# A fused macaron block in fp32: the last attention projections and one more kept pair as Strassen-Winograd block products

## The chip, the cores and the metric

The kernel runs on one core of a Trainium2 chip. The metric is the device time of one execution in microseconds; lower is better. Several executions are timed and the median is given.

## The reference

Four sequences of 1024 tokens with 1024 channels, all in fp32: 4096 tokens, or 32 tiles of 128. A gated feed-forward part is added with half weight, then attention, then the same feed-forward part again. Cut to what matters:

```python
def ffn(x):                                  # x: 4096 x 1024
    dots = softmax(x @ centroids.T / 0.1)    # 64 clusters
    hits = dots > 0.01
    dense = x @ weight.T + bias              # 1024 x 1024
    row_sel = any(hits, axis=0)[assignments] # which output columns are kept
    return where(any(hits, axis=1)[:, None] & row_sel[None, :], dense, 0)

def attn(x):                                 # 32 query heads, 8 key/value heads, width 32
    q, k, v = x @ Wq + bq, x @ Wk + bk, x @ Wv + bv
    k, v = repeat(k, 4), repeat(v, 4)
    scores = einsum('bsdh,bseh->bsde', q, k) / sqrt(32)
    return einsum('bsde,bseh->bsdh', softmax(scores), v)

x = x + 0.5 * ffn(layernorm(x))
x = x + attn(layernorm(x))
x = x + 0.5 * ffn(layernorm(x))
```

The scores of a token are taken between its own channels d and e, summed over the heads; no token attends to another one. A column is kept only if some token anywhere hits its cluster, so the mask of each feed-forward part is known only when all 32 tiles have been through its gate.

## The kernel before

The work is in tiles of 128 tokens. `wc` holds W.T and the centroids side by side, 1024 + 64 columns; the last part of a product (columns 768 to 1088, 320 wide) holds the last 256 outputs and the 64 logits of the gate. `wqkv` holds the projection, 768 columns, the four query heads of a group already summed.

There are three stages, in an order of instructions that is written out by hand: each engine executes its own in the order of the program.

The first stage makes the first feed-forward part and stores its rows in DRAM (`d1`). The second is the loop over `s` from 0 to 36 (line 982), a software pipeline. I call one pass *step s*. In it tile s is projected, tile b = s - 2 has its scores (L877), softmax and weighted sum (`attend`, L919), tile g = s - 3 gets the attention added by GpSimd (`second_added`, L944 and L948) and its layernorm moments by VectorE (L162), tile f = s - 4 is transposed for the last part (L205), and tile a = s - 5 goes through the gate (`gate_2`: a product of 320 columns, L212). The third stage makes the rest of the last feed-forward part and writes the result.

Two tiles can share a matrix product in the Strassen-Winograd form: their rows are split into halves over the contraction, and the weights into four blocks of 512 x 384. Seven products of blocks then do the work of eight. `project_two` (L801) does so for the projections of the steps in `PAIRED`, `winograd` (L284) for the feed-forward part. Both are generators: each `next` emits one product and its adds, so that they can be interleaved with other work. They need sums of token blocks (`token_sums`, four GpSimd instructions at L257 to L260) and of weight blocks (`weight_sums`, L245).

The weight sums of the projection (`qts`) lie in the first 768 columns of `wc`, so W.T itself waits in DRAM (`wtd`) and comes back by four transfers on SP's queue (L989), each of 768 KB. Before, two are issued at the top of step 29 and two at the top of step 30. The weight sums of the last feed-forward part (`ts`) in turn lie in `wqkv`, and VectorE makes them in steps 32 and 33.

The six last tiles, 26 to 31, are *kept*: their x, xT and feed-forward rows stay on the chip. Tiles 26 and 27 are finished by `rest` in steps 32 and 33, one tile in each by two plain products; 28/29 by `winograd` in steps 34 and 35, 30/31 in stage 3.

Some orders matter here. All products of this stage but scores and weighted sums take their PSUM bank from one tag of four (`bank`). Scores and weighted sums share one buffer (`att`). In a paired odd step the gathers of the new tile (`rearranged`, L845 and L851) stand ahead of the attention's store (L935) and return (L940) on SP's queue; in an unpaired step behind. In an odd paired step whose follower is also paired, two gates run; in the others after the start, one. The gates are closed by this:

```python
def gates_used():
    for a in sorted(es):
        gated(es.pop(a), a, 1)
```

It runs in each odd or unpaired step, ahead of the softmax.

Of the kernel before, what the change touches and what calls it, by code (L numbers as in the profile page):

```python
# [33 lines left out]
KEPT = 6  # L34
LAST = 2 * HALF, (EMB + NCL) // 2 - HALF
GATED = range(8, 28)
PAIRED = range(4, 30)
WARM = 16
ROWS = 26

# [2 lines left out]
def kernel(  # L43
# [39 lines left out]
    nc = tc.nc  # L83
    xf = x.flatten_outer_dims()
    of = out.flatten_outer_dims()
    NT = xf.shape[0] // P
# [20 lines left out]
    for base, sign in ((0, 1), (HKV - 1, -1)):  # L107
        nc.gpsimd.affine_select(
            out=tq,
            in_=tq,  # L110
# [9 lines left out]
    wc = const.tile([P, KT, EMB + NCL], F32, name="wc")  # L120
# [14 lines left out]
    xt, dt_, xT = {}, {}, {}  # L135
# [79 lines left out]
    def ffn_part(src, i, dst, name, biased=True):  # L215


        lo, hi = PARTS[i]
        p = product(src, wc, lo, hi, f"ff_{name}_{i}")
        hi = min(hi, EMB)  # L220
        if biased:
            nc.vector.tensor_tensor(dst[:, lo:hi], p[:, : hi - lo], brow[:, lo:hi], ALU.add)
        else:
            nc.scalar.copy(dst[:, lo:hi], p[:, : hi - lo])
        return p[:, hi - lo : hi - lo + NCL] if i == 2 else None

    def rest(t):

        for i in range(2):
            ffn_part(xT[t], i, dt_[t], f"3_{t}")  # L230
        del xT[t]

    def blocks(wts, lo=0, n=HALF):

        return [
            wts[:, 4 * i : 4 * i + 4, lo + h * n : lo + (h + 1) * n] for i in (0, 1) for h in (0, 1)
        ]

    def weight_sums(ws, ts, engines):

        w11, w12, w21, w22 = ws
        t1, t2, t3, t4 = ts
        sums = (t1, w12, w11), (t2, w22, t1), (t3, w22, w12), (t4, w21, t2)
        for engine, (o, p, q) in zip(engines, sums):
            engine.tensor_tensor(o, p, q, ALU.subtract)  # L245
            yield
# [214 lines left out]
    def first_added(t):  # L461
        masked(dt_[t], t, 0, mask)
        nc.gpsimd.tensor_tensor(xt[t], xt[t], dt_.pop(t), ALU.add)  # L463
# [6 lines left out]
    with (  # L470
# [5 lines left out]
        ts = [stage.tile([P, 4, HALF], F32, tag=f"ws{i}", name=f"ws{i}") for i in range(4)]  # L476
# [286 lines left out]
    with (  # L763
# [129 lines left out]
        def weighted(s, t, between=lambda: None):  # L893


            st = attn.tile([P, NBLK, 4, D], F32, tag="stt", name=f"stt{t}")
            nc.vector.transpose(
                st.rearrange("p b t d -> p (b t d)"), s.rearrange("p b t e -> p (b t e)")
            )
            between()  # L900
            sm = small.tile([P, 2, 4, 4], F32, tag="asm", name=f"asm{t}")
            nc.vector.tensor_reduce(
                sm.rearrange("p m i t -> p i m t"),
                s.rearrange("p (i m) t e -> p i m t e", m=2),
                AX.X,
                ALU.add,
            )
            rs = small.tile([P, D], F32, tag="rs", bufs=3, name=f"rs{t}")
            nc.vector.transpose(rs, sm.rearrange("p m i t -> p (m i t)"))
            nc.vector.reciprocal(rs, rs)  # L910
            return st, rs
# [44 lines left out]
        def has(t):  # L956
            return 0 <= t < NT
# [13 lines left out]
        def gate_2(a):  # L971
            if a not in dt_:
                dt_[a] = row(f"d3_{a}")
            es[a] = gate(ffn_part(xT[a], 2, dt_[a], f"3_{a}", biased=a >= FIRST_KEPT), a, 1)
# [4 lines that stand above are left out]
                if a < FIRST_KEPT:  # L979
                    store_2(a)  # L980

        for s in range(NT + 5):
            b, g, f, a = s - 2, s - 3, s - 4, s - 5
            paired, odd = s in PAIRED, s % 2 == 1
            if has(s + 4):
                load_2(s + 4)
            for i in {PAIRED.stop - 1: (0, 1), PAIRED.stop: (2, 3)}.get(s, ()):

                nc.sync.dma_start(out=blocks(wc)[i], in_=wtd[i])  # L989
            if has(b):  # L990
                sc = scores(qkv[b][0], kd.pop(b), b)
            if has(b):
                nc.scalar.activation(sc, sc, AF.Exp, scale=QK_SCALE)
            if paired:
                if not odd:
                    two = project_two(s, s + 1, ss2)
                next(two)
            if has(s + 1) and s + 1 not in xT2:
                xT2[s + 1] = transposed(xn2.pop(s + 1), f"2_{s + 1}")
            if has(s - 1):  # L1000
                kd[s - 1] = keys(qkv[s - 1][0], s - 1)
            if has(g):
                second_added(ot.pop(g), rs.pop(g), g)
            if g >= 0 and g < FIRST_KEPT:
                nc.gpsimd.dma_start(out=y2[g], in_=xt[g])
            if odd or not paired:
                gates_used()
            if 3 <= s <= 4:
                next(qsums)
            if has(s + 2):  # L1010
                normal = sums_normed(xt[s + 2], f"2_{s + 2}")
                next(normal)
            if paired and not odd:
                next(two)
            if has(b):
                st, rs[b] = weighted(sc, b, lambda: next(two) if paired and odd else None)
            if paired and not odd:
                first_added(s + 3)
                next(two)
            if has(s + 2):  # L1020
                xn2[s + 2] = next(normal)
            if paired and not odd:
                next(two)
            if paired and odd and s + 1 in PAIRED:
                gate_2(a)
                xT[f] = transposed(xn3.pop(f), f"3_{f}")
            if paired and (not odd or s + 1 not in PAIRED):
                fo = attend(st, qkv.pop(b)[1], b)
            if s == NT + 2:
                dt_[a] = row(f"d3_{a}")  # L1030
                steps = winograd(s - 6, s - 5, ss, ts, None, 3)
                for _ in range(3):
                    next(steps)
            if has(g):
                mv = moments(xt[g], f"3_{g}")

            def between():
                if has(s + 3) and s + 3 in dt_:
                    first_added(s + 3)
                if has(g):  # L1040
                    xn3[g] = normed(xt[g], mv, f"3_{g}")

            if paired:
                if not odd:
                    next(two)
                between()
            elif has(s):
                flat[s] = project(xT2.pop(s), s, between)
            else:
                between()  # L1050
                k = s - NT
                if k < 2:
                    rest(s - 6)
                    if k == 0:
                        sums = weight_sums(blocks(wc), ts, [nc.vector] * 4)
                    for _ in range(2):
                        next(sums)
                if k > 2:
                    load_xT(k - 3)
                if 2 <= k < 4:  # L1060
                    for _ in range(1 if k == 2 else 3):
                        next(steps)
            if paired and odd:
                qkv[s] = rearranged(flat.pop(s), s)
            if has(b) and b in qkv:
                fo = attend(st, qkv.pop(b)[1], b)
            if s in flat:
                qkv[s] = rearranged(flat.pop(s), s)
            if has(b):
                ot[b] = returned(fo, b)  # L1070
            if has(s - 1):
                qkv[s - 1] = (qkv[s - 1][0], values(qkv[s - 1][1], s - 1))
            if has(f) and f in xn3:
                xT[f] = transposed(xn3.pop(f), f"3_{f}")
            if odd and s + 1 in PAIRED:
                xT2[s + 2] = transposed(xn2.pop(s + 2), f"2_{s + 2}")
                ss2 = token_sums(xT2, s + 1, s + 2, "2q")
            if 1 <= s <= 3:

                for _ in range(2 if s == 1 else 1):  # L1080
                    next(held[s // 2])
                i = {1: NT - 4, 3: NT - 2}.get(s)
                for i in (i, i + 1) if i else ():
                    nc.sync.dma_start(out=d1[i], in_=dt_.pop(i))
            if s == 1:
                next(qsums)
            if s == NT + 1:
                ss = token_sums(xT, f - 1, f, 2)
                asg = load_assigned()
            if s == NT + 3:  # L1090
                hot = one_hot(asg)
            if paired:
                if odd:
                    gate_2(f if s + 1 in PAIRED else a)
            elif has(a) and a not in es:
                gate_2(a)
            for i in sorted(es) if odd or not paired else ():
                es[i] = gate_exp(es[i], i, 1)
# [118 lines left out]
```

## Time and profile before

| | us |
|---|---|
| median of 3 runs | 1323.7 (1322.91 to 1324.2) |
| the profiled execution | 1323.88 |
| its span | 1322.2 |
| TensorE busy | 1301.0 |
| VectorE busy | 871.0 |
| GpSimd busy | 583.3 |
| ScalarE busy | 495.1 |
| step 29 begins (scores on TensorE) | 941.22 |
| step 32 begins | 993.12 |
| step 33 begins | 1010.98 |
| step 34 begins | 1028.72 |

Times in the rows are microseconds from the span's start. A row of a timeline gives the start, the length, the engine (PE is TensorE, DVE VectorE, ACT ScalarE, POOL GpSimd, SPq the DMA issues of SyncE), the line of the kernel, the operation, what it writes and reads, and how many instructions are merged in it; in brackets stands the idle time of the engine just before, with what ended it. An fp32 matmul of the program is two instructions in the rows, so a product of four blocks shows as x8.

### The profile page before, as it was taken

Reading aid. Unit: us, or ns where it says so; the run is one execution under the profiler, and the core shown is the slowest. Engines: PE = TensorE matmul, PEld = TensorE weight load, DVE = VectorE, ACT = ScalarE, POOL = GpSimd, SP = SyncE. Lnnn points to the kernel's source line nnn. Section 1 sums busy time; section 2 is a strip of 40 time slices with the busy share of each in tenths; the row PEclk is TensorE's granted clock in tenths of the full one; section 3 lists DMA queues with packets and bytes.
Section 4 is the critical chain, followed back from the end, with each engine's and each line's share of the span. In section 5 each row is a group of like instructions: output and inputs, shape, how many; then the busy total and the mean of one; then the engine's idle time right before and its main releaser. Section 6 shows DMA issues by size and latency. Waiting matters only on the chain.

```text
span 1322.2 us, 22786 instructions
## 1 busy us (share of the span) xinstructions
PE 1301.0 (98%) x8726; PEld 840.5 (64%) x8726; DVE 871.0 (66%) x1789; ACT 495.1 (37%) x821; POOL 583.3 (44%) x448
## 2 busy tenths in 40 slices
PE   8998999999999999999999999999999999999998
PEld 7664677777776665666666666666666655555554
DVE  4655555555546358888888888778867448555556
ACT  4432223333210445666666666666643200000000
POOL 3621132232112147566666666666532326634440
PEclk9999899999999999999999999999999999999999
DMA  8487876778614155456666665665551346655532
GB/s 297 86 161 146 170 146 139 167 180 173 124 64 191 43 166 160 153 191 189 195 200 195 189 198 166 200 200 189 163 156 26 104 139 227 239 200 176 178 114 80
DMA packets 296301, 214.25 MB, mean 162 GB/s; under 512 B 240064, under 2 KB 255168, under 8 KB 296192
## 3 DMA queue, kind: packets, MB, share of 16 engines
q1 hardware_dynamic: 278240, 164.78, 46.5%
q0 software_dynamic: 8736, 30.68, 6.3%
q10 hardware_dynamic: 9216, 17.33, 3.6%
q8 instruction: 69, 1.13, 0.4%
q14 instruction: 40, 0.33, 0.1%
HBM read 127.77 MB, written 84.96 MB: 161 GB/s over the span
## 4 chain that ended last, share of the span: by engine, by line
PE 93%; DMA 2%; DVE 2%; ACT 1%; issue 1%; POOL 0%; SPq 0%; ACTq 0%; POOLq 0%; DVEq 0%
PE st L284 40%; PE qs L801 18%; PE ff L212 16%; PE la L348 6%; PE tp L205 4%; PE pq L212 4%; PE sc L877 2%; PE po L919 2%; DMA x<-in_L_attn_x_dram 1%; DVE bn L162 1%; DMA scd<-sc 1%; PE tpw L558 0%; DMA qkvd<-qkv 0%; DMA xb<-in_L_attn_x_dram 0%; DVE d L275 0%
## 5 line engine op out<-in xcount | busy, mean ns | idle before, releaser
L212 PE MATMUL ff<-wc,xT 128*128 128x320 f32 (+1 forms) x768 | 218.1, 438 | 1.7 <-ACT wc L563 0.7
L212 PEld LDWEIGHTS ff<-wc,xT 128*128 128x128 f32 x768 | 143.7, 190 | 64.1 <-ACT xT L206 1.0
L257 POOL TENSOR_TENSOR ts<-xT 128x512 f32<-128x512 f32 x31 | 41.4, 1335 | 309.6 <-DVE xT L509 172.7
L284 PE MATMUL st<-wc,xT 128*128 128x384 f32 x496 | 170.5, 487 | 0.0
L275 DVE TENSOR_TENSOR d<-st,d 128x384 f32<-128x384 f32 x157 | 86.1, 550 | 109.8 <-PE st L284 108.5
L284 PE MATMUL st<-ws,ts 128*128 128x384 f32 x384 | 131.2, 486 | 0.9 <-DVE d L275 0.9
L857 POOL TENSOR_TENSOR kd<-qk,tmask 128x1024 f32<-128x1024 f32 x32 | 60.6, 1893 | 161.9 <-DMA qk<-qkvd 144.5
L284 PEld LDWEIGHTS st<-wc,xT 128*128 128x128 f32 x496 | 93.3, 191 | 60.4 <-issue 1.3
L284 PE MATMUL st<-wqkv,ts 128*128 128x384 f32 x360 | 121.3, 486 | 0.0
L162 DVE BATCH_NORM_STATS2 bn<-x 128x6 f32<-128x512 f32 x132 | 84.3, 680 | 40.4 <-DMA x<-in_L_attn_x_dram 38.2
L801 PE MATMUL qs<-wc,ts_2q 128*128 128x384 f32 x312 | 106.2, 490 | 0.0
L452 DVE SCALAR_TENSOR_TENSOR d<-d,qsel,mask 128x1024 f32<-128x1024 f32 (+2 forms) x68 | 102.8, 1512 | 0.1
L463 POOL TENSOR_TENSOR x<-x,d 128x1024 f32<-128x1024 f32 x32 | 75.5, 2358 | 59.5 <-DVE d L452 46.6
L165 ACT ACTIVATE mv<-mv,eps 128x1 f32<-128x1 f32 x66 | 19.4, 295 | 219.6 <-DVE mv L164 213.1
L284 PEld LDWEIGHTS st<-ws,ts 128*128 128x128 f32 x384 | 71.1, 190 | 44.2 <-issue 2.2
L284 PEld LDWEIGHTS st<-wqkv,ts 128*128 128x128 f32 x360 | 68.3, 190 | 48.1 <-issue 0.8
L275 DVE TENSOR_TENSOR d<-st,brow 128x384 f32<-128x384 f32 x93 | 51.3, 551 | 56.6 <-PE st L284 56.5
L284 PE MATMUL st<-wc,ts 128*128 128x384 f32 x248 | 85.1, 486 | 0.0
L206 ACT COPY xT<-tp 128x512 f32<-128x512 f32 x138 | 73.1, 581 | 30.8 <-PE tp L205 29.9
L801 PEld LDWEIGHTS qs<-wc,ts_2q 128*128 128x128 f32 x312 | 58.2, 190 | 40.5 <-issue 2.6
L948 POOL TENSOR_TENSOR x<-x,ot 128x1024 f32<-128x1024 f32 x32 | 78.1, 2442 | 2.5
L205 PE MATMUL tp<-ident,xn 128*128 128x128 f32 x552 | 73.0, 275 | 3.2 <-ACT xn L180 1.7
(143 smaller groups left out, 2248.2 us busy)
## 6 DMA issues: line engine op xcount, KB each, us to landing
x<-in_L_attn_x_dram SPq DMA_DIRECT2D x64, 512.0 KB, 4.6
d<-d SPq DMA_DIRECT2D x64, 512.0 KB, 4.8
out_dram<-x ACTq DMA_DIRECT2D x30, 512.0 KB, 4.7
xb<-in_L_attn_x_dram SPq DMA_DIRECT2D x108, 128.0 KB, 5.0
y<-x POOLq DMA_DIRECT2D x26, 512.0 KB, 3.1
xTd<-xT POOLq DMA_DIRECT2D x26, 512.0 KB, 5.7
xT<-xTd SPq DMA_DIRECT2D x26, 512.0 KB, 4.9
x<-y SPq DMA_DIRECT2D x26, 512.0 KB, 5.1
```

The costliest lines, as they stand in the source:

```text
L162: nc.vector.bn_stats(st[:, i, :], src[:, i * 512 : (i + 1) * 512])
L205: nc.tensor.transpose(tp[:, j, :], xn[:, k * P : (k + 1) * P], ident)
L206: nc.scalar.copy(t_[:, 4 * h : 4 * h + 4, :], tp)
L212: nc.tensor.matmul(p, src[:, k, :], wts[:, k, lo:hi], start=(k == 0), stop=(k == KT - 1))
L275: nc.vector.tensor_tensor(out, ps, other, ALU.add)
L284: nc.tensor.matmul(ps, src[:, k, :], wts[:, k, :], start=(k == 0 and onto is None), stop=(k == 3), skip_group_check=onto is not None,)
L348: nc.tensor.matmul(ps, src[:, k, :], wts[:, k, :], start=(k == 0 and onto is None), stop=(k == 3), skip_group_check=onto is not None,)
L452: nc.vector.scalar_tensor_tensor(d[:, sl], d[:, sl], qsel[which][:, t : t + 1], mask[:, sl], ALU.mult, ALU.mult)
L463: nc.gpsimd.tensor_tensor(xt[t], xt[t], dt_.pop(t), ALU.add)
L801: nc.tensor.matmul(ps, src[:, k, :], wts[:, k, :], start=(k == 0 and onto is None), stop=(k == 3), skip_group_check=onto is not None,)
L857: nc.gpsimd.tensor_tensor(kd, qk[:, :, D:].unsqueeze(2).to_broadcast([P, NBLK, 4, D]), tmask.unsqueeze(1).unsqueeze(3).to_broadcast([P, NB ...
L948: nc.gpsimd.tensor_tensor(xv, xv, ov, ALU.add)
```

## The change

The projections of tiles 30 and 31 are made by `project_two`, as those of the pairs before them, and the feed-forward part of the kept pair 26/27 by `winograd` in place of `rest`. Two of W.T's blocks now come back at the top of step 31, two behind its softmax. The token sums of 26/27 and the first two weight sums are made at the end of step 31, the other two in step 32. The first product of `winograd` in steps 32 and 33 is emitted between the scores and the softmax; three more follow in step 32 and two more in step 33. Gates 24 and 25 both run in step 29, gates 26 and 27 both in step 31. The core of the diff:

```diff
-PAIRED = range(4, 30)
+PAIRED = range(4, 32)
...
-    def rest(t):
-        for i in range(2):
-            ffn_part(xT[t], i, dt_[t], f"3_{t}")
-        del xT[t]
...
+        def returns(*some):
+            for i in some:
+                nc.sync.dma_start(out=blocks(wc)[i], in_=wtd[i])
...
-            for i in {PAIRED.stop - 1: (0, 1), PAIRED.stop: (2, 3)}.get(s, ()):
-                nc.sync.dma_start(out=blocks(wc)[i], in_=wtd[i])
+            if s == NT - 1:
+                returns(1, 0)
             if has(b):
                 sc = scores(qkv[b][0], kd.pop(b), b)
...
+            if NT <= s < NT + 2:
+                next(steps)
             if has(b):
                 st, rs[b] = weighted(sc, b, lambda: next(two) if paired and odd else None)
+            if s == NT - 1:
+                returns(3, 2)
             if paired and not odd:
-                first_added(s + 3)
+                if has(s + 3):
+                    first_added(s + 3)
                 next(two)
...
-            if paired and odd and s + 1 in PAIRED:
+            if paired and odd:
                 gate_2(a)
                 xT[f] = transposed(xn3.pop(f), f"3_{f}")
-            if paired and (not odd or s + 1 not in PAIRED):
+            if paired and not odd:
                 fo = attend(st, qkv.pop(b)[1], b)
...
                 k = s - NT
                 if k < 2:
-                    rest(s - 6)
-                    if k == 0:
-                        sums = weight_sums(blocks(wc), ts, [nc.vector] * 4)
+                    for _ in range(3 - k):
+                        next(steps)
+                if k == 0:
                     for _ in range(2):
                         next(sums)
...
+            if s == NT - 1:
+                ss = token_sums(xT, f - 1, f, 2)
+                steps = winograd(f - 1, f, ss, ts, None, 3)
+                sums = weight_sums(blocks(wc), ts, [nc.vector] * 4)
+                for _ in range(2):
+                    next(sums)
...
             if paired:
                 if odd:
-                    gate_2(f if s + 1 in PAIRED else a)
+                    gate_2(f)
             elif has(a) and a not in es:
                 gate_2(a)
```

## The prediction

> **What bounds the kernel now.** I read the page's busy rows and its chain first, then TensorE's timeline from step 27 to step 34, then the VectorE, SyncE and GpSimd timelines of the same steps, then the waits.
>
> ```profile
> PE 1301.0 (98%) x8726; PEld 840.5 (64%) x8726; DVE 871.0 (66%) x1789; ACT 495.1 (37%) x821; POOL 583.3 (44%) x448
> PE 93%; DMA 2%; DVE 2%; ACT 1%; issue 1%; POOL 0%; SPq 0%; ACTq 0%; POOLq 0%; DVEq 0%
> ```
>
> TensorE works 98% of the span and carries 93% of the chain. A change gains what it takes off TensorE and loses each wait that it gives TensorE. TensorE's rows (start, length, line, work, idle before it):
>
> ```profile
> 955.82 0.66 PE L205 MATMUL tp<-ident,xn 128*128 128x128 f32 x4
> 957.94 0.66 PE L205 MATMUL tp<-ident,xn 128*128 128x128 f32 x4 [1.47 <-ACT xT L206]
> 958.43 10.58 PE L212 MATMUL pq<-wqkv,xT 128*128 128x384 f32 x32
> 968.95 1.07 PE L919 MATMUL po<-stt,vt 32*32 32x128 f32 x64
> ...
> 993.12 1.07 PE L877 MATMUL sc<-kd,qk 32*32 32x128 f32 x64
> 994.12 10.59 PE L212 MATMUL ff<-wc,xT 128*128 128x384 f32 x32
> 1004.64 1.07 PE L919 MATMUL po<-stt,vt 32*32 32x128 f32 x64
> 1005.64 1.09 PE L205 MATMUL tp<-ident,xn 128*128 128x128 f32 x8
> 1006.57 4.47 PE L212 MATMUL ff<-wc,xT 128*128 128x320 f32 x16
> 1010.98 1.06 PE L877 MATMUL sc<-kd,qk 32*32 32x128 f32 x64
> ```
>
> Each step opens with the scores row: 993.12 opens step 32, 1010.98 step 33. A plain product of a whole tile costs 968.95 - 958.43 = 10.52 us (32 instructions), a gate 4.41. There is no wait in steps 32 and 33. VectorE in step 32 (first rows, then those around the middle):
>
> ```profile
> 994.23 1.23 DVE L886 TENSOR_REDUCE amx<-sc 128x32 f32<-128x1024 f32 x1
> ...
> 1000.79 1.22 DVE L162 BATCH_NORM_STATS2 bn<-x 128x6 f32<-128x512 f32 x2
> ...
> 1002.95 0.55 DVE L222 TENSOR_TENSOR d<-ff,brow 128x384 f32<-128x384 f32 x1
> ...
> 1005.22 1.75 DVE L245 TENSOR_TENSOR wqkv<-wc 128x1536 f32<-128x1536 f32 x1
> 1007.00 1.76 DVE L245 TENSOR_TENSOR wqkv<-wc,wqkv 128x1536 f32<-128x1536 f32 x1
> ```
>
> VectorE finishes its last read of `po` at 1010.63, 0.35 us before the next scores overwrite that buffer: TensorE's cover over VectorE is thin here.
>
> **The change, part by part.** *Projections 30/31.* Two plain products (2 x 10.52 = 21.04) become seven block products. In steps 28 and 29 those take 10.52 + 2.68 + 2.68 + 2.72 = 18.60. The 1.47 us wait before the transposes of 31 goes: they move to the end of step 29, as at 919.72 in step 27, where nothing is waited for. The cover there is that of the steady state (xn copied on ScalarE, four token sums at 1.27 each on GpSimd, ready at 929.46 for use at 929.70); if it failed, the sums would cost up to the 1.47 that went. Steps 29, 30 and 31 take the lengths of steps 27 (18.78) and 28 (16.17), and of 27 less its two transposes for later tiles (0.87 + 0.93), 16.98. So step 32 starts at 941.22 + 51.93 = 993.15 against 993.12: no gain yet, but gate 27 (4.41) is already done.
>
> *Gate 27 twice.* `gates_used` empties `es` at the top of step 32, so `a not in es` holds for a = 27 at its end, and `gate_2(27)` runs again. This is 16 instructions, 4.41 us on TensorE, and on VectorE 0.42 + 0.21 + 0.28 and four small ones (0.65). What the earlier gate saved is paid back in step 32.
>
> *Kept pair 26/27.* Step 32 holds four block products, 10.52 as before. Step 33 holds three, 7.74 by the run from 1044.96 to 1052.70, in place of 10.52. TensorE alone, without waits: step 32 ends at 1011.0 and step 33 at 1011.0 + 17.74 - 2.78 = 1026.0 where it was 1028.72. That is -2.75 us. All later steps are unchanged on TensorE; the eight adds of the pair where there were four lie on VectorE.
>
> *VectorE at the end of step 31.* Two weight sums (1005.22 to 1008.68, 3.46 us) now stand ahead of gate 27 and the softmax of step 32. I shifted step 29's rows by 34.95 us. Gate 26 is done at 987.9, the moments of 28 and their scales at 990.2, the `po` rows and the value transpose at 992.6, the sums at 996.0, gate 27 at 996.9. So amx starts at 997.0, 2.8 later than 994.23 in its step. To the moments were 6.56 us; add one more gate's use (0.65, less the wait of 0.36 on the exponential that it fills) and the first product's add (0.5): moments at m = 1004.05 on VectorE's own account, not 1000.79.
>
> *W.T back.* Four SP transfers of 768 KB move from steps 29 and 30 to step 31. Two stand ahead of the store of qkv 31 and two behind it; past them must go the gathers of 31 (one for q and k, four for v), then, in a paired odd step, the store of o 29 and the return of ot 29. GpSimd's second add of 29 needs that ot, and the moments of 29 need its x. No row shows four blocks in one step. From the nearest rows: the store of qkv 31 issues at 949.18 + 34.95 = 984.1 and lands 7.5 later (as in step 29, also behind two blocks): 991.6. The q/k gather issues then (0.4) and the v gathers take 4.89 of SP, as in step 27 (2.06 when the queue is quiet). So o 29 goes out at 997.0, lands after 4.4 (925.62 to 929.99 in step 27), ot after 2.15, and the GpSimd rows take 0.8 and 2.36: x at 1006.75, m = 1006.85. With quiet rows (v 2.06, o 2.4) x would come at 1001.9 and VectorE's own 1004.05 would rule. I take the step 27 rows, since step 31 has more in flight, not less. The upper end is a block more (2.6 us from 5.1 to 7.7 between two landings): m = 1009.5. The blocks themselves: block 3 is needed by the second sum at 994.3, block 2 by the third product at 999.3; by the rows they land about 995 and 998, under the same lateness.
>
> ```profile
> DMA to landing us min/median/max: 5.1/6.4/7.7
> ```
>
> The Trainium skill, "DMA: Bandwidth & Descriptors", section "Anatomy of one DMA — SWDGE (gpsimd) path", fits 2.0 us plus bytes over 436 GB/s: 3.8 us for a block, 2.3 for o. By it x comes 2.1 earlier, m = 1004.75, and the sum below would be +0.75. The rows (5.1 and 7.7 us) say slower, and they decide.
>
> *GpSimd.* Gates 24 and 25 now both run in step 29, so their four stores (1.28 MB, 0.54 to 0.6 of GpSimd each) leave together in step 31, behind the second add of 28 (done at 987.7) and ahead of the token sums of 26/27, which are new here: four by 1.27, so the first is ready at 991.2 and the second at 992.4. The products that read them start at 996.7 and 1001.9: hidden, with 5 us to spare. If the stores held GpSimd up for longer than that, the excess would go to TensorE. The four more adds of the pair 30/31 on VectorE (0.5 each) lie in steps whose likes, 27 and 28, have no TensorE wait.
>
> *What m does.* After the moments VectorE needs 2.2 to the scales and then makes four adds, ending m + 2.7, 3.2, 3.75, 4.2. The PSUM banks come back in order of last use: in step 34 ff waits at 1040.55 for the add ending 1040.49, which read the second product. So in step 32 the second half of the transposes takes the bank of the third product (m + 2.7) and gate 27 that of the second (m + 3.75). With m = 1006.85, gate 27 starts at 1010.6 instead of 1006.57. VectorE then makes the sums (3.46) and the four `po` rows (2.0): m + 9.7 = 1016.55, when the scores of step 33 may start, against 1011.0. In step 33 the return of ot 30 follows from there as in step 32 before, and ff 28's bank is free when reached. Step 34 starts at 1016.6 + 14.96 = 1031.55: **+2.8 us**. The rule is m - 1004.0.
>
> The first product put behind the scores costs TensorE nothing and saves nothing: its own queue had no work between these anyway. The effect is its add, 0.5 us ahead of the softmax, counted in m.
>
> **A wait that halves the clock.** In stage 1 a wait of 4.00 us was followed by a product of 5.49 instead of 2.74, at a granted clock of 0.50; after a wait of 2.32 the product took 2.85 at 1.00.
>
> ```profile
> 110.50 2.85 PE L284 MATMUL st<-ws,xT 128*128 128x384 f32 x8 [2.32 <-DVE d L275]
> ...
> 133.92 5.49 PE L284 MATMUL st<-ws,xT 128*128 128x384 f32 x8 [4.00 <-DVE d L275]
> ```
>
> The Trainium skill, "TensorE: Matmul & The Clock Gate", section "Part 1: The HAM clock gate (the "warmup" mystery)", has the clock fall after an idle window of about 3.4 us, free-running. My wait before the transposes is m + 2.7 - 1006.1 = 3.45 us, then 0.5. A window lies wholly in it only by luck, so I leave the clock at 1.00. If it falls, add 2.7 us: the sum would be +5.5.
>
> **Sum.** The profiled execution took 1323.88 (span 1322.2 and 1.68 around it), 0.18 over the median 1323.7. 1323.88 + 2.8 = 1326.7.
>
> **The rivals.** *Transfers in time* (0.14): only VectorE's own lateness, m = 1004.05; 0.0, from -1.5 to +1.5. For it: SP has no loads left after step 27. *Later still, or the clock halves* (0.22): m about 1009 or 2.7 more; +4.5 to +8. For it: the row at 133.92, and 3.1 MB to be moved beside 1.28 MB of GpSimd's stores. *The cover holds* (0.09): VectorE is not late. It decides at m = 1001.2, below which no wait is left; price -2.75, and -3.2 with the 0.47 us wait of step 34 gone, 1320.7 to 1321.1. Against it: 3.46 us of sums ahead of a softmax that left 0.35. *Gate 27 does not run twice* (0.03): the change then does what it says, and 4.4 us come off step 32: about -1.6 with the waits, -7 without.
>
> **How the numbers follow.** My forecast, the wait at m between 1005.5 and 1008.3 (+1.5 to +4.3), has 0.52; of it 0.35 lies above +2.65 us (0.2%, about what a measurement of this kernel tells from no change) and 0.17 below. Slower: 0.35 + 0.22 = 0.57. Same: 0.17 + 0.14 = 0.31. Faster: 0.09 + 0.03 = 0.12. The range runs from the cover that holds, 1321.0, to a wait with a block's delay or the clock's fall, 1331.0. The likeliest case's own range is 1325.4 to 1328.2.
>
> **What would show it.** Right: 16 more ff instructions of 320 columns less 64 of 384 (L212); no pq after step 3; a wait of TensorE of 2 to 4 us in step 32 on the transposes, released by VectorE's `d` adds, and about 1.5 before the scores of 33; the moments of 29 released by GpSimd's x. Wrong: TensorE's rows in steps 32 and 33 with no idle time, ot 29 landed before 1002, or a single gate of 27.

## The result, and the profile after

The change makes the kernel slower: the median of the changed kernel is 1329.58 us (1325.47 to 1332.53, 20 runs), that of the kernel before in the same comparison 1325.39 (1322.43 to 1329.0, 20 runs). The ratio is 1.0031, 95% interval 1.0021 to 1.004, or 4.2 us at 1325.

The profiled execution of the changed kernel took 1325.47 us with a span of 1323.8. It is the quickest of its 20 runs, so spans are not to be compared: before step 29 it was 3.1 us ahead of the profile of before (its step 29 begins at 938.08, not 941.22) in work that both kernels share. A shorter stay at a low clock and a shorter wait in stage 1, at 133 us, make 1.8 of that, and a shorter wait for a transfer at 505 us makes 1.3. What the change did is read from the stretch that it touches, from the start of step 29 to the start of step 34:

| | before, us | after, us |
|---|---|---|
| steps 29 to 31 | 51.90 | 52.89 |
| step 32 | 17.86 | 23.33 |
| step 33 | 17.74 | 16.01 |
| the stretch | 87.50 | 92.23 |

The stretch is 4.7 us longer, of which step 32 takes 5.5. The page's row of busy time shows none of it:

```profile
PE 1300.0 (98%) x8726; PEld 840.1 (63%) x8726; DVE 879.2 (66%) x1804; ACT 495.2 (37%) x823; POOL 593.2 (45%) x456
```

TensorE has as many instructions as before: 8 fewer for each of the two pairs, 16 more for the second gate of tile 27. TensorE's timeline (start, length, line, work, idle before it and what ended it; lines are six lower than before in this part) shows where it stood still:

```profile
977.51 2.85 PE L795 MATMUL qs<-wc,xT 128*128 128x384 f32 x8 [0.65 <-DVE qkv L828]
...
990.97 1.07 PE L871 MATMUL sc<-kd,qk 32*32 32x128 f32 x64
...
1001.25 2.82 PE L278 MATMUL st<-wqkv,ts 128*128 128x384 f32 x8 [1.27 <-DVE d L269]
...
1007.30 0.66 PE L205 MATMUL tp<-ident,xn 128*128 128x128 f32 x4 [1.64 <-DVE d L269]
1008.35 4.58 PE L212 MATMUL ff<-wc,xT 128*128 128x320 f32 x16 [0.40 <-DVE d L269]
1014.30 1.06 PE L871 MATMUL sc<-kd,qk 32*32 32x128 f32 x64 [1.38 <-DVE o L925]
...
1025.89 4.58 PE L212 MATMUL ff<-wc,xT 128*128 128x320 f32 x16 [0.57 <-DVE d L269]
```

Step 32 runs from 990.97 to 1014.30. Its four waits sum to 4.69 us, all on VectorE; before there was none. VectorE in the same step:

```profile
990.49 2.32 DVE L239 TENSOR_TENSOR wqkv<-wc 128x1536 f32<-128x1536 f32 x1
992.85 2.70 DVE L239 TENSOR_TENSOR wqkv<-wc,wqkv 128x1536 f32<-128x1536 f32 x1
...
999.08 0.93 DVE L408 SCALAR_TENSOR_TENSOR best<-ge,gsm,best 128x64 f32<-128x64 f32 x1
...
1004.48 1.29 DVE L162 BATCH_NORM_STATS2 bn<-x 128x6 f32<-128x512 f32 x2 [0.48 <-POOL x L942]
...
1012.52 1.52 DVE L925 SCALAR_TENSOR_TENSOR o<-po,tmask,o 128x256 f32<-128x256 f32 x3
```

The moments of 29 start 13.51 us after the step, not 7.67 as before, and all that stands behind them moves with them: the adds that give the banks back, and the last read of `po`, ending at 1014.0, which releases the scores of step 33. The 0.48 tells that two things arrived almost together there: VectorE was free at 1004.0, and x at 1004.45. GpSimd and SyncE:

```profile
991.15 2.79 POOL L254 TENSOR_TENSOR ts<-xT,ts 128x512 f32<-128x512 f32 x1
...
1001.28 0.73 POOL L938 TENSOR_TENSOR ot<-ot,rs 128x256 f32<-128x256 f32 x1 [1.35 <-DMA ot<-od]
1002.09 2.36 POOL L942 TENSOR_TENSOR x<-x,ot 128x1024 f32<-128x1024 f32 x1
```

```profile
981.90 1.25 SPq L979 DMA_DIRECT2D wc<-wtd  x2
988.50 0.38 SPq L839 DMA_DIRECT2D qk<-qkvd  x1
988.93 7.10 SPq L845 DMA_DIRECT2D v<-qkvd  x4
996.07 0.45 SPq L929 DMA_DIRECT2D od<-o  x1
999.10 0.34 SPq L934 DMA_DIRECT2D ot<-od  x1
```

The four v gathers hold SP for 7.10 us behind W.T's blocks (2.06 in a quiet queue), and the store of o 29, ready since 990.2, leaves at 996.07.

### The profile page after: what moved, and what is told of

Its sections match the earlier page's. It is cut to its first block, busy times and chain, and to the rows that moved or that the text cites. A ratio compares the mean times of both kernels' runs of the same rounds, so it can differ in the third digit from the quotient of the medians.

```text
span 1323.8 us, 22814 instructions
## 1 busy us (share of the span) xinstructions
PE 1300.0 (98%) x8726; PEld 840.1 (63%) x8726; DVE 879.2 (66%) x1804; ACT 495.2 (37%) x823; POOL 593.2 (45%) x456
## 3 DMA queue, kind: packets, MB, share of 16 engines
q8 instruction: 69, 1.13, 0.4%
## 4 chain that ended last, share of the span: by engine, by line
PE 92%; DVE 3%; DMA 3%; ACT 1%; issue 1%; POOL 0%; SPq 0%; DVEq 0%; ACTq 0%; POOLq 0%
PE st L278 40%; PE qs L795 20%; PE ff L212 14%; PE la L342 6%; PE tp L205 4%; PE pq L212 2%; PE sc L871 2%; PE po L913 2%; DMA x<-in_L_attn_x_dram 1%; DMA scd<-sc 1%; DVE bn L162 1%; DVE d L269 1%; DMA od<-o 0%; PE tpw L552 0%; DVE wqkv L239 0%
## 5 line engine op out<-in xcount | busy, mean ns | idle before, releaser
L212 PE MATMUL ff<-wc,xT 128*128 128x320 f32 x720 | 201.7, 433 | 2.7 <-DVE d L269 1.4
L278 PE MATMUL st<-wc,xT 128*128 128x384 f32 x512 | 175.8, 486 | 0.0
L212 PEld LDWEIGHTS ff<-wc,xT 128*128 128x128 f32 x720 | 134.8, 190 | 59.0 <-DVE d L269 2.1
L278 PEld LDWEIGHTS st<-wc,xT 128*128 128x128 f32 x512 | 96.0, 190 | 62.0 <-issue 0.6
L278 PE MATMUL st<-wqkv,ts 128*128 128x384 f32 x384 | 129.7, 487 | 1.3 <-DVE d L269 1.3
L795 PE MATMUL qs<-wc,ts_2q 128*128 128x384 f32 x336 | 114.4, 490 | 0.0
L278 PEld LDWEIGHTS st<-wqkv,ts 128*128 128x128 f32 x384 | 72.7, 190 | 52.8 <-issue 2.8
L795 PEld LDWEIGHTS qs<-wc,ts_2q 128*128 128x128 f32 x336 | 62.7, 190 | 43.6 <-issue 2.8
L278 PE MATMUL st<-wc,ts 128*128 128x384 f32 x256 | 87.8, 486 | 0.0
L795 PE MATMUL qs<-wqkv,xT 128*128 128x384 f32 x224 | 78.3, 492 | 0.0
```

Of the source, the lines that this page charges most:

```text
L212: nc.tensor.matmul(p, src[:, k, :], wts[:, k, lo:hi], start=(k == 0), stop=(k == KT - 1))
L278: nc.tensor.matmul(ps, src[:, k, :], wts[:, k, :], start=(k == 0 and onto is None), stop=(k == 3), skip_group_check=onto is not None,)
L795: nc.tensor.matmul(ps, src[:, k, :], wts[:, k, :], start=(k == 0 and onto is None), stop=(k == 3), skip_group_check=onto is not None,)
```

## The experiments

The lengths in the table are read from the profile of one execution of each kernel; the ratio is that of all the times to those of the kernel before. Moments: start of the moments of 29, counted from the start of step 32.

| kernel | stretch | step 32 | step 33 | moments | ratio (95%) |
|---|---|---|---|---|---|
| before | 87.50 | 17.86 | 17.74 | 7.67 | |
| changed | 92.23 | 23.33 | 16.01 | 13.51 | 1.0031 (1.0021 to 1.004) |
| kept_only | 89.87 | 19.47 | 16.50 | 9.69 | 0.9994 (0.9984 to 1.0004) |
| proj_only | 95.22 | 24.56 | 17.75 | 14.86 | 1.0039 (1.0027 to 1.0051) |
| gate_once | 94.83 | 24.45 | 17.48 | 14.62 | 1.0035 (1.0019 to 1.0051) |
| o_first | 95.51 | 26.20 | 16.41 | 16.36 | 1.0053 (1.0035 to 1.0072) |
| returns_early | 92.92 | 23.54 | 16.48 | 13.77 | 1.0031 (1.002 to 1.0042) |
| early_t1_gp | 87.39 | 18.39 | 15.18 | 10.07 | 0.9995 (0.9985 to 1.0004) |
| whole_mended | 88.31 | 16.51 | 17.83 | 10.08 | 0.9989 (0.9977 to 1.0001) |
| kept_gpsimd | 85.10 | 18.02 | 15.17 | 9.70 | 0.9978 (0.997 to 0.9987) |
| sums34_gp | 91.77 | 23.70 | 15.17 | 14.07 | 1.0029 (1.0019 to 1.0039) |
| first_plain | 104.57 | 28.80 | 22.86 | 14.12 | 1.0109 (1.0084 to 1.0134) |

**kept_only: the kept pair alone.**

```diff
 # on the kernel before (PAIRED stays range(4, 30), W.T back in steps 29 and 30)
-                    rest(s - 6)
+                    for _ in range(3 - k):
+                        next(steps)
+            if NT <= s < NT + 2:        # behind the scores
+                next(steps)
+            if s == NT - 1:
+                dt_[f] = row(f"d3_{f}")
+                ss = token_sums(xT, f - 1, f, 2)
+                steps = winograd(f - 1, f, ss, ts, None, 3)
+                sums = weight_sums(blocks(wc), ts, [nc.vector] * 4)
+                for _ in range(2):
+                    next(sums)
```

> The kept pair alone: the kernel before, with 26/27 by block products (first product behind the scores, token sums and two weight sums at the end of step 31, the other two in step 32); pairs 30/31 stay plain, W.T comes back in steps 29 and 30, gate 27 runs once in step 32. Theory (the block products themselves pay; the loss comes from what was moved into step 31): VectorE was idle for 2.94 us at the end of step 31, so the sums find room, the moments of 29 come about 1 us later in step 32, TensorE waits for less than 1 us, and step 33 is 2.5 us shorter: the stretch from step 29 to step 34 goes from 87.5 to about 85.5, the time to about 2 us less than before. Rival (the adds and sums of the kept pair make VectorE late by themselves): waits of 3 to 4 us in step 32 as in the changed kernel, the stretch at 88.5 to 90, the time 1 to 2.5 us more than before.

Measured: no change in the time (0.9994), between the two expectations. The moments came 2.0 us later than before, not 1, and step 32 and 33 together took 35.97 us where before they took 35.60: what the block products save went into two waits.

```profile
1012.32 1.06 PE L871 MATMUL sc<-kd,qk 32*32 32x128 f32 x64 [1.38 <-DVE o L925]
...
1024.40 4.58 PE L212 MATMUL ff<-wc,xT 128*128 128x320 f32 x16 [1.07 <-DVE d L269]
```

Here x of 29 was in time, so this is VectorE's own lateness: its two sums took 2.31 and 2.71 us beside GpSimd's token sums (1.75 and 1.76 before). The moments started at 9.69, the scores of step 33 at 19.47: 9.78 later, as the prediction's m + 9.7. The stretch holds 2.0 us that are no part of this: in step 30 the clock fell after a wait of 1.85 us (1.47 before), and the plain product there took 12.07 instead of 10.58.

**proj_only: the projections alone.**

```diff
 # on the changed kernel
-            if NT <= s < NT + 2:
-                next(steps)
...
-                    for _ in range(3 - k):
-                        next(steps)
-                if k == 0:
+                    rest(s - 6)
+                    if k == 0:
+                        sums = weight_sums(blocks(wc), ts, [nc.vector] * 4)
                     for _ in range(2):
                         next(sums)
...
-            if s == NT - 1:             # token sums, winograd, two weight sums
```

> The projections alone: the changed kernel, with 26/27 by plain products and the weight sums in steps 32 and 33 as before; W.T back in step 31 and gate 27 twice as in the change. Theory (what step 31 does to the transfers costs the time): x of 29 still comes 13.5 us after step 32 begins, because ot 29 stands behind four blocks; the one add that the bank of gate 27 needs comes behind it, step 32 takes about 22 in place of 17.9, step 33 gains nothing: stretch about 92.5 to 93, about 5 us more than before. Rival (the weight sums ahead of gate 27 cost it): without them VectorE is in time, step 32 takes 18, the stretch is 88.5, and the time is 1 us more than before.

Measured: 1.0039, 5.0 us more than before, the size that the theory had. VectorE was ready for the moments at 999.3 and stood still for x:

```profile
1006.38 1.29 DVE L162 BATCH_NORM_STATS2 bn<-x 128x6 f32<-128x512 f32 x2 [7.11 <-POOL x L948]
```

But the wait that TensorE shows is another, for a block of W.T itself, which the expectation had overlooked:

```profile
998.88 10.94 PE L212 MATMUL ff<-wc,xT 128*128 128x384 f32 x24 [3.51 <-DMA wc<-wtd]
```

The plain product wants block 2 one product earlier than the block products do. It waited 3.51 us for it, and then ran at a granted clock of 0.50 until about 1004: 10.94 us for what takes about 7.9 at full clock. Had the block been in time, about 1 us would have been won (an estimate from VectorE's rows), for VectorE's last read of `po`, set by the late x, ended at 1015.8, and the scores of step 33 began at 1016.08:

```profile
1014.30 1.52 DVE L931 SCALAR_TENSOR_TENSOR o<-po,tmask,o 128x256 f32<-128x256 f32 x3
```

So with VectorE unburdened, the transfers put into step 31 cost as much as the whole change, by two roads that end together, and this run does not tell their shares apart. In the changed kernel TensorE waits for no block.

**gate_once: gate 27 run once.**

```diff
-            elif has(a) and a not in es:
+            elif has(a) and s != NT:
```

> The changed kernel, with the second run of gate 27 taken out. Theory (VectorE's last read of po sets the start of step 33): TensorE gets 4.4 us of its work back and waits instead, about 6 us before the scores of step 33; the scores start no earlier, the stretch stays at 92.2, and if the clock falls in that wait it grows to 94 or 95. Rival (the second gate is simply TensorE work): the stretch falls by 4.4 to 87.8, the time by 4.4.

Measured: 1.0035, the same as the changed kernel. TensorE waited in place of the gate, and the clock fell in the wait:

```profile
1014.77 1.52 PE L871 MATMUL sc<-kd,qk 32*32 32x128 f32 x64 [6.35 <-DVE o L925]
1016.22 4.70 PE L278 MATMUL st<-wqkv,ts 128*128 128x384 f32 x8
```

The product after it took 4.70 us where 2.74 is usual. Work that is wasted cost nothing here, because it filled a wait. The moments came 1.1 us later in this profile than in the changed kernel's: VectorE's second weight sum waited 1.71 us for a block of W.T, and x too came later. What decides is the distance from the moments to the scores, 9.83 us with the gate once and 9.82 with it twice.

**o_first: the weighted sums of 29 ahead of the gathers of 31 on SP's queue.**

```diff
-            if paired and odd:
+            if paired and odd and s != NT - 1:
                 qkv[s] = rearranged(flat.pop(s), s)
...
-            if s in flat:
+            if s in flat and s != NT - 1:
                 qkv[s] = rearranged(flat.pop(s), s)
             if has(b):
                 ot[b] = returned(fo, b)
+            if s in flat:
+                qkv[s] = rearranged(flat.pop(s), s)
```

> The changed kernel, with the weighted sums of 29 stored and fetched back ahead of the gathers of 31 in step 31. Theory (two delays of equal size end together: VectorE is free for the moments of 29 only 0.48 us before x arrives): x comes 3 to 4 us earlier, the moments only 0.5, the stretch falls by 0.5 to 91.7. Rival (the transfers alone hold step 32): the stretch falls by 3.5 to 88.7.

A miss on both sides: it made things worse (1.0053), and x came later, not earlier.

```profile
993.61 0.38 SPq L929 DMA_DIRECT2D od<-o  x1
1001.73 0.33 SPq L934 DMA_DIRECT2D ot<-od  x1
```

The store of o 29, sent out at 993.61, released its return only at 1001.73: 8.1 us, where a quiet queue takes 2.4. It queued behind the last two blocks just the same, and now the gathers of 31 waited behind it, and GpSimd's keys of 31, which stand ahead of its second add of 29, waited for them (7.73 us). So the order of what follows does not help against what is already under way. VectorE's second weight sum also waited for a block, and it was made while GpSimd stood idle; it took 1.76, where the changed kernel's took 2.70:

```profile
998.59 1.76 DVE L239 TENSOR_TENSOR wqkv<-wc,wqkv 128x1536 f32<-128x1536 f32 x1 [3.01 <-DMA wc<-wtd]
```

**returns_early: two of the four blocks sent for in step 30.**

```diff
-            if s == NT - 1:
-                returns(1, 0)
...
                     first_added(s + 3)
                 next(two)
+                if s == NT - 2:
+                    returns(1, 0)
```

> The changed kernel, with the first two blocks of W.T sent for in step 30, right behind the product that reads the last sum kept in their place, so that only two blocks are in the way in step 31. Theory (two delays end together): x of 29 comes at about 9 to 10 us after step 32 begins, not 13.5, but VectorE itself is not free for the moments before 13.0; the moments move by 0.5 and the stretch from step 29 to step 34 from 92.2 to 91.7. Rival (the transfers alone hold step 32): the moments move by 3.5, the stretch goes to 88.7 and the time 3.5 below the changed kernel's.

Measured: 1.0031, no gain, as the theory of two delays has it. GpSimd's add ended 9.8 us after the start of step 32, and VectorE came to the moments only at 13.77, now waiting for nothing:

```profile
1002.90 2.35 POOL L942 TENSOR_TENSOR x<-x,ot 128x1024 f32<-128x1024 f32 x1
```

```profile
1009.24 1.22 DVE L162 BATCH_NORM_STATS2 bn<-x 128x6 f32<-128x512 f32 x2
```

(Step 32 begins at 995.47 in this kernel.) The 0.5 us that were expected did not come, since GpSimd, now busy earlier, held VectorE longer: its sums took 2.66 and 2.71, and the small row 1.42.

**early_t1_gp: both delays taken away, and the last two sums made by GpSimd.** The edit of returns_early, and:

```diff
             if s == NT - 1:
                 returns(3, 2)
+                sums = weight_sums(blocks(wc), ts, [nc.vector] * 2 + [nc.gpsimd] * 2)
+                next(sums)
...
-                sums = weight_sums(blocks(wc), ts, [nc.vector] * 4)
-                for _ in range(2):
-                    next(sums)
+                next(sums)
```

> The run with two blocks sent for in step 30, and besides VectorE relieved: its first weight sum stands in its idle 2 us of step 31 (ahead of gate 26), and the last two sums are made by GpSimd. The second run of gate 27 stays. Theory (both delays gone): moments of 29 at about 10.7 us after step 32 begins, the bank of the second gate free at 14.5, scores of step 33 at 18.9, step 33 about 15.5: stretch 87.3, about what it was before the change. Rival (TensorE's bank waits have yet another cause): stretch stays above 90.

Measured: stretch 87.39 (87.3 was expected), ratio 0.9995: the whole loss of the change is gone. The moments were at 10.07, the scores of step 33 at 18.39. Of the 4.9 us that step 32 got shorter, 3.4 lie ahead of the moments (the two delays) and 1.5 between them and the scores (the sums that GpSimd now makes). What is left is the second gate, and a new wait of 0.84 before the scores of step 32.

**whole_mended: the same with gate 27 once.**

```diff
-            elif has(a) and a not in es:
+            elif has(a) and s != NT:
```

> The same, and gate 27 run once. Theory (with VectorE in time, what the second gate costs on TensorE comes back in part; then VectorE's last read of po, about 6.3 us behind the moments, opens step 33): scores of step 33 at about 17 us after step 32 begins, stretch 85.4, time 2 us below the kernel before and 6 below the changed one. Rival (TensorE is the only bound left): scores at 13.5, stretch 81.5, time 6 us below the kernel before. Other rival (gate 27's second run is hidden): no less than the run with it.

Measured: scores of step 33 at 16.51 (17 expected), but the ratio of 0.9989 (0.9977 to 1.0001) is not clear of no change. The theory's gain in step 32 came and was given back in step 33, where the clock had fallen:

```profile
1011.29 1.51 PE L871 MATMUL sc<-kd,qk 32*32 32x128 f32 x64 [2.92 <-DVE o L925]
1012.74 5.06 PE L278 MATMUL st<-wqkv,ts 128*128 128x384 f32 x8
```

5.06 for a product of 2.74, and 0.5 for the scores: 2.8 us, as much as the wait itself.

**kept_gpsimd: the kept pair alone, its last two weight sums by GpSimd.**

```diff
 # on kept_only
-                sums = weight_sums(blocks(wc), ts, [nc.vector] * 4)
+                sums = weight_sums(blocks(wc), ts, [nc.vector] * 2 + [nc.gpsimd] * 2)
```

> The kept pair alone, as in the first run of that kind (kernel before, 26/27 by block products), with the last two weight sums made by GpSimd. Theory (3.5 us of sums ahead of the last read of po made the waits of 1.38 and 1.07 there): the scores of step 33 start at TensorE's own pace, 17.9 us after step 32, step 33 is 15.1: stretch about 85.0, time 2.5 us below the kernel before. Rival (GpSimd's second add of 30[...] takes the place): stretch 87.5 to 88.5, time no less than before.

Measured: stretch 85.10 (85.0 expected) and a median of 1323.26 against 1325.62: ratio 0.9978 (0.997 to 0.9987), 2.4 us less and the fastest of all. Both waits of kept_only are gone:

```profile
1007.90 4.57 PE L212 MATMUL ff<-wc,xT 128*128 128x320 f32 x16
1012.41 1.07 PE L871 MATMUL sc<-kd,qk 32*32 32x128 f32 x64
```

The moments start as late as in kept_only (9.70); only what stands between them and the last read of `po` has changed.

**sums34_gp: that one edit on the changed kernel.**

```diff
-                sums = weight_sums(blocks(wc), ts, [nc.vector] * 4)
+                sums = weight_sums(blocks(wc), ts, [nc.vector] * 2 + [nc.gpsimd] * 2)
```

> The changed kernel with one edit: the last two weight sums are made by GpSimd. Theory (VectorE's queue behind the moments of step 32 holds the scores of step 33): the moments stay at 13.5 us after step 32 begins, the waits on the banks stay (together about 3.3), but the last read of po comes 3.4 earlier, so the 1.4 us wait before the scores goes and also the 0.6 in step 33: stretch from step 29 to step 34 from 92.2 to about 90.2. Rival (the moments alone decide): stretch 92. Other rival (GpSimd's sums now come late for the first product of step 33): stretch above 92.

The waits before the scores of step 33 and before ff 28 went, as expected; step 33 took 15.17. But the stretch was 91.77, and the ratio of 1.0029 does not differ from the changed kernel's. The two waits on the banks stayed (1.52 and 1.69, within 6 us), and this time the clock fell after them: gate 27's second run took 5.82 us instead of 4.58. The window view (length; busy time and instructions of TensorE, its weight loads, VectorE, ScalarE, GpSimd; granted clock; DMA share; GB/s):

```profile
1012.00:1014.00 2.00, 1.79 (x6) 1.20 (x7) 1.95 (x5) 1.98 (x4) 2.00 (x2) 0.58 0.00 0
```

Taking that off, the stretch would be 90.5, near the expected 90.2. That is an estimate, since no execution of this kernel without the fall was profiled. As measured, the number is that of the first rival (92); only the rows speak for the theory.

**first_plain: the first product emitted with the others.**

```diff
-            if NT <= s < NT + 2:
-                next(steps)
...
-                    for _ in range(3 - k):
+                    for _ in range(4 - k):
                         next(steps)
```

> The changed kernel with the first product of steps 32 and 33 emitted with the others, behind the softmax and the moments, not behind the scores. TensorE's order is the same. Theory (what this part of the change moves is VectorE's add that reads the first product: the fourth product is accumulated onto the same bank and cannot start before that add): the add then stands behind the moments, the fourth product starts at about 16 us after step 32 begins instead of 10.3, a wait of 6 us in which the clock may fall, and step 32 takes 26 in place of 23.3: stretch 95 or more. Rival, as the prediction had it (that placing costs TensorE nothing and saves nothing, VectorE's softmax only comes 0.5 earlier): stretch 91.7 to 92.2.

Measured: 1.0109, far the slowest, in the theory's direction and beyond its size. The medians are 1341.49 and 1324.44, 17.0 us apart, and the stretch is 17.1 longer than before.

```profile
1013.21 4.58 PE L278 MATMUL st<-wqkv,ts 128*128 128x384 f32 x8 [7.60 <-DVE d L269]
```

The fourth product waits 7.60 us, until the add that reads the first one, then runs at a fallen clock (4.58); step 33 has the same again with 5.65.

## Why the prediction was right or wrong

*Right: direction, place and mechanism.* The loss lies in step 32; TensorE waits for VectorE's adds and for its last read of `po`, and the moments of 29 set both. They were put at 13.7 us after the step's start and came at 13.51; the scores of step 33 were put at 23.4 and came at 23.33. The rule "m + 9.7" held in the kernels that kept the four sums on VectorE and the first product behind the scores (9.70 to 9.84; first_plain, without that placing, has 14.7).

*That 13.7 came so close is in part luck.* Counted from the start of step 32, the gathers of 31 began 0.9 us sooner than put. The four v gathers held SP for 7.10 us and not 4.89, and the return of ot 29 left 3.0 us after its store and not 4.4. These errors cancelled. To take the rows rather than the fit that the prediction quotes was right: the fit gave 3.8 us for a block, and the four landed 4.8 to 14.2 us after their issue. The section quoted is on transfers that GpSimd sends, and these are SP's.

*Why m was late: half right.* The prediction gave two accounts, VectorE's own (m = 10.9 after the step's start) and the transfers' (13.7), and let the later rule. In fact both ended together: VectorE was free at 13.0, x came at 13.5. The step that failed is "the sums at 996.0": 3.46 us for two sums was the price without company. Beside GpSimd's new token sums they took 5.02, and one small VectorE row that usually takes 0.28 took 0.93. The prediction had counted the token sums as hidden, and looked only at who waits for them. (Its sum is also 0.3 us short: 997.0 with its own terms 6.56, 0.65 - 0.36 and 0.5 gives 1004.35, not 1004.05.) returns_early (half of the transfers out of the way, no gain) and kept_only (no transfers in the way, still 2 us late) show VectorE's delay, and proj_only (VectorE ready 7.11 us before x) shows that of the transfers; early_t1_gp, with both gone and two sums moved to GpSimd, gives 4.8 us of stretch back.

*Wrong: "costs TensorE nothing and saves nothing"* of the first product behind the scores. The fourth product is accumulated onto the first one's bank, so it needs the add that reads the first. Even in the changed kernel that was a wait of 1.27 us which the prediction did not have; without the placing it is 7.60, and the time 1341.49. In the changed kernel that wait did not lengthen the step, since the scores follow the moments; it came off the wait before the transposes, which was put at 3.45 and was 1.64. This part of the change is what made the rest bearable.

*Wrong: the price of the second gate.* It does run twice (720 instructions of 320 columns, 704 before), but "what the earlier gate saved is paid back in step 32" does not hold in the changed kernel: gate_once shows that without it the scores start no earlier. The rival that put a single gate at -1.6 is refuted too.

*Mis-sized:* steps 29 to 31 were to take 51.93 and took 52.89. With the transposes of later tiles gone, nothing stands between the last two products of the pair, and the second waits 0.65 us for the add that reads the first. Step 33 was to take 14.96 and took 16.01, 0.57 of it a wait for the return of ot 30, which took 3.7 us after its store where it took 2.4 before; why is open. These two terms make the difference between +2.8 and the stretch's +4.7. The medians differ by 4.2; the predicted 1326.7 stood on one execution (1323.88) close to a median of three (1323.7), and that of twenty is 1325.39.

*The clock* was left at 1.00, and in the profile of the changed kernel it stayed there in step 32. That was no test of the reason given, since the wait of 3.45 us did not occur. The kernel's other 19 executions were not profiled, so it is open whether their clock fell in step 32, as that of sums34_gp did after waits of 1.52 and 1.69 us. Over the 14 runs of whole_mended and the 9 of gate_once the mean granted clock was 0.9947 and 0.993; over 20 of the changed kernel 0.996, as for the kernel before (0.995 to 0.996).

*Not tried:* the changed kernel with GpSimd's token sums taken away from VectorE's sums in time, all else equal. That they are what lengthens the sums rests on the rows: 1.75 when GpSimd is idle (1.76 in o_first, in the same step), 2.3 to 2.7 when it runs, and GpSimd's own row 2.79 instead of 1.27 at the same moment. Nor was it tried to move GpSimd's four stores of gates 24 and 25 (1.28 MB), which leave at 985.1 to 987.3, beside W.T's blocks. From 985 to 994 the DMA engines were busy all the time (share 1.00 to 1.06), so how much of the transfers' lateness is due to the blocks and how much to the stores is open.

## What to carry to other kernels

When TensorE is busy 98% of the time, ask what each other engine must have finished by the time TensorE returns to a buffer, and count the whole queue ahead of that instruction; a saving on TensorE of 2.6 us was worth nothing until 3.5 us of sums were moved out of VectorE's queue (kept_gpsimd, with 0.9978). If two delays end together, removing either shows no gain: try both before calling one of them harmless. Work given to an engine with time to spare can still stand in the way of another: the token sums on GpSimd made VectorE's two sums 1.6 us longer. And look for the accumulation that reuses a bank: the read in between belongs as early in its queue as the product is.

## What the runs showed of the hardware

The length of a wait alone did not decide whether the granted clock fell. One wait stands in stage 1 of every kernel here, in work that no edit touches: TensorE waits 2.31 or 2.32 us for an add of VectorE (at 110.50 in the profile of before). In three of the twelve profiles the product behind it took 2.85 us (before, the changed kernel, sums34_gp), in the other nine 4.36 to 4.54. So the row that the prediction took from before was one of the three. The clock also fell after a wait of 1.85 us (kept_only, step 30), after two of 1.52 and 1.69 us with little work between (sums34_gp, clock 0.58), and after one of 2.92 (whole_mended); it did not fall after 2.46, 2.72 and 3.23 us in stage 1 (proj_only, gate_once, kept_only), nor after 1.27 and 1.64 in the changed kernel. After each of the fourteen waits of 3.5 us or more that these profiles hold behind their first 20 us, it fell. In the stretch a fall after 1.5 to 3.5 us of waiting cost 1.2 to 3.0 us, not much less than the wait.

A VectorE row that reads two arrays from SBUF and a GpSimd one lengthened each other: 1.75 to 2.7 and 1.27 to 2.8 us when they met. The ends show that they took turns. In the changed kernel GpSimd's third token sum ended at 991.19; VectorE's sum, begun at 990.49, ended 1.62 us after that, GpSimd's next row 1.13 us after VectorE's, and VectorE's second sum 1.61 us after GpSimd's. Each is about what the row takes alone. The small row of 0.93 ended at 1000.01, when GpSimd's keys had ended at 999.93. In o_first the sum and the GpSimd row began within 0.01 us of each other, and only one of them paid: VectorE's kept 1.72, GpSimd's took 2.85. VectorE's moments, which read one array, kept 1.22 beside a sum of GpSimd (kept_gpsimd).

A transfer of 128 KB with two blocks of 768 KB ahead on its queue and GpSimd's stores beside it took 8.1 us from issue to the release of its return (2.4 in a quiet queue), and four small gathers held the issuing engine for 7.1 us.
